# Two GATv2 layers on one core: where a few edges are added up, and which engine divides the sums

## The chip, the cores and the metric

The kernel runs on one core of a Trainium2 chip. The core has five engines that run their own instruction streams and meet at semaphores: PE (TensorE, the matmuls; PEld is its weight load), DVE (VectorE), ACT (ScalarE), POOL (GpSimd, which here issues the indirect DMAs) and SP (SyncE, which issues plain DMAs). The metric is the device time of one execution, in microseconds (us). The kernel before takes 3889.89 us, the median of three runs (3889.52 to 3891.73).

## What is computed

A graph has 6250 nodes with 256 features and 100000 edges, sorted by target. Two GATv2 layers (4 heads of 64) with an ELU between them, a residual and a layer norm; then one GAT layer (8 heads of 32), a residual and a layer norm. Cut to what matters here:

```python
def _gatv2_layer(x, src, dst, n, Wl, Wr, att, b):
    xl = (x @ Wl).reshape(n, H, C)
    xr = (x @ Wr).reshape(n, H, C)
    e = jax.nn.leaky_relu(xl[src] + xr[dst], NEG_SLOPE)
    logits = jnp.einsum('ehc,hc->eh', e, att)
    m = jax.ops.segment_max(logits, dst, num_segments=n)
    ex = jnp.exp(logits - m[dst])
    denom = jax.ops.segment_sum(ex, dst, num_segments=n)
    alpha = ex / (denom[dst] + 1e-16)
    msg = xl[src] * alpha[:, :, None]
    out = jax.ops.segment_sum(msg, dst, num_segments=n)
    return out.reshape(n, H * C) + b
...
h = _gatv2_layer(x, src, dst, n, Wl1, Wr1, att1, b1)
h = jax.nn.elu(h)
h = _gatv2_layer(h, src, dst, n, Wl2, Wr2, att2, b2)
```

In each GATv2 layer every node also has an edge to itself.

## The kernel before

**Blocks.** The nodes are sorted by their number of incoming edges, the largest first, and cut into 49 blocks of 128; a node has a partition. Block b has cols[b] columns, and column j holds the j-th source of each of its nodes. The number of columns falls from block to block: with the node's own row, the blocks have S = 28 at first and 10 at last in the first two layers. Three loops over the 49 blocks follow one another, one for each layer; the first two are calls of layer2 (i = 0 and 1).

**Columnless edges.** In block 0 a few nodes have more edges than cols[0]. These FEW further places a node are the columnless edges: their logits and their share of the sum are worked out for all of them together, an edge to a partition, and brought to their nodes and back by products with two matrices of zeros and ones, node_of and edges_of. few_r (L1513) brings the target's row to the edges; few_logits gives their logits to lg; few_sum (L1293) brings the weights to the edges (few_w, L1298), weighs the edges' rows on DVE (L1303 to L1307) and adds them to block 0's sum `acc` with a last matmul (L1311).

**One block of a GATv2 layer.** POOL gathers a row of the table for each node and column (L1235), one indirect DMA to a column, into tiles `g` of up to nine columns; there are nine such tiles, so POOL can be some blocks ahead, until it has to wait for a tile that PE has not read yet. own() gives the node's own two rows (layer 1: a transpose and two products on PE, `pl` and `pr`, copied by ACT; layer 2: loaded, copied by ACT). attend(b) has three DVE instructions for each tile: `z` (L1504, L1505) and the sum over a head's features into `lg` (L1506). weights() takes the largest logit of each head on DVE (`top`, L1374), and then ACT does an exponential a head with the sum of its results (`wt` and `den`, L1381). DVE takes the reciprocal (`den`, L1571). weighted_sum multiplies the rows by the weights: most columns on DVE (L1411), the last few on ACT, one instruction a column and head (L1410). PE adds the columns up with matmuls by the identity into `acc` in PSUM (L1418). There is one `acc` (pool ps1 with one buffer), and there are two buffers of `wt`.

**The end of a block lies in the next one.** In iteration b the loop does the gathers of block b+1 and own(b+1), then attend(b), then end(b-1): DVE multiplies block b-1's `acc` by its reciprocals in one instruction (L1537), adds the bias (layer 1, L1542) and hands on to finish1 or finish2. finish1 has the ELU on ACT (L1609 to L1612) and DVE (L1617), a transpose, products, two copies on ACT (L1624) and two stores on SP; finish2 the residual, the statistics and the layer norm (L1464), then a transpose, a product, copies and a store.

**Order.** Every engine does its instructions in the order in which the program has them. On ACT an iteration is thus: the copies of own(b+1), the exponentials of b, a copy of the weights that ACT itself uses (`by`), own's other copy, the spots of the sources (L1530, layer 1), end(b-1)'s part, L1410, and the copies at the end of finish. On DVE: `z` and `lg`, `top`, in the first blocks of layer 1 the sorting of sources (sort_sources), L1537 and what follows, `den`, L1411. On PE: own(b+1), the sum of b, then finish of b-1.

In block 0, few_r stands after all of the block's `z` and `lg`, and few_sum directly after the block's sum: `more` is called at the end of weighted_sum.

Of the kernel before, what the change touches and what calls it, by code (L numbers as in the profile page):

```python
# [26 lines left out]
F32 = mybir.dt.float32  # L27
# [8 lines left out]
P = 128  # L36
# [1106 lines left out]
def tile_by_degree(  # L1143
# [3 lines left out]
    nc = tc.nc  # L1147
    N, F = x.shape
    H2, D2 = att1.shape
    H1, _, D1 = w3.shape  # L1150
    NB = -(-N // P)
# [3 lines left out]
    W2 = H2 * (D2 + 1)  # L1155
# [9 lines left out]
    def per_head(t, H):  # L1165
        return t.rearrange("p (h d) -> p h d", h=H)
# [24 lines left out]
    node_of = consts.tile([P, P], F32, name="node_of")  # L1191
# [204 lines left out]

        return (wt, None), add_up

    def weighted_sum(ps, rows, cut, wts, H, width, between, more=None):

        wt, by = wts
        acc = ps.tile([P, F], F32, name="acc")
        S = cut[-1][1]
        for g, (s0, s1) in zip(rows, cut):
            n = s1 - s0
            g4 = g[:, :n, : H * width].rearrange("p t (h d) -> p t h d", h=H)[:, :, :, : F // H]
            m = n - by.shape[1] if by is not None and s1 == S else n
            for t in range(m, n):
                for h in range(H):
                    nc.scalar.mul(g4[:, t, h, :], g4[:, t, h, :], by[:, t - m, h : h + 1])  # L1410
            nc.vector.tensor_mul(  # L1411
                g4[:, :m], g4[:, :m],
                wt[:, s0 : s0 + m, :].unsqueeze(3).to_broadcast([P, m, H, F // H]),
            )
            if s0 == 0:
                between()
            for t in range(n):
                nc.tensor.matmul(  # L1418
                    acc, ident, g4[:, t], start=s0 + t == 0, stop=s0 + t == S - 1 and not more
                )  # L1420
        if more:
            more(acc, wt, S)
        return acc

    def added_up(work, prod, rows, cut, wts, H, width, between):
# [40 lines left out]
    def layer2(i, table, of, width, start, own, finish, follow):  # L1466

        with ExitStack() as es:
            zp = es.enter_context(tc.tile_pool(name=f"z{i}", bufs=1))
            work = es.enter_context(tc.tile_pool(name=f"work{i}", bufs=3))
            ps = es.enter_context(tc.tile_pool(name=f"ps{i}", bufs=2, space=PSUM))
            ps1 = es.enter_context(tc.tile_pool(name=f"ps1{i}", bufs=1, space=PSUM))
            pst = es.enter_context(tc.tile_pool(name=f"pst{i}", bufs=2, space=PSUM))
            at = ps1.tile([P, W2], F32, name="at")
            nc.scalar.copy(at, att[i])
            state = {}  # L1480

            def gather(b):
                first = EARLY[b] if b in begun else 0
                rows, cut = begun.pop(b) if first else row_tiles(b, 1)
                gather_rows(b, rows, cut, 1, table, of, width, first, cols[b])
                if b == 0:
                    gather_few(table, i, width)
                state[b] = [rows, cut]

            later = []  # L1490

            def ready(b):
                pr, put = own(work, ps, pst, b, state[b][0][0][:, 0, :W2])
                state[b].append(pr)
                later.append(put)

            def attend(b):
                rows, cut, xr = state.pop(b)
                S = cols[b] + 1
                lg = work.tile([P, CM + 1, H2], F32, name="lg")  # L1500
                for g, (s0, s1) in zip(rows, cut):
                    n = s1 - s0
                    z = zp.tile([P, T, W2], F32, name="z")[:, :n, :]
                    nc.vector.tensor_max(z, g[:, :n, :W2], xr[:, None, :].to_broadcast([P, n, W2]))  # L1504
                    nc.vector.tensor_mul(z, z, at[:, None, :].to_broadcast([P, n, W2]))  # L1505
                    nc.vector.reduce_sum(  # L1506
                        lg[:, s0:s1, :], z.rearrange("p t (h d) -> p t h d", h=H2), axis=AX.X
                    )
                if b == 0:
                    own_r = work.tile([P, W2], F32, name="few_own", bufs=1)  # L1510
                    nc.scalar.copy(own_r, xr)
                    po = pst.tile([P, W2], F32, name="few_r", tag="tp")
                    nc.tensor.matmul(po, node_of, own_r, start=True, stop=True)  # L1513
                    none(po)
                    z = zp.tile([P, T, W2], F32, name="z")[:, 0, :]
                    nc.vector.tensor_max(z, few_row[:, :W2], po)
                    nc.vector.tensor_mul(z, z, at)
                    few_lg = work.tile([P, H2], F32, name="few_lg", bufs=1)
                    nc.vector.reduce_sum(few_lg, per_head(z, H2), axis=AX.X)
                    few_logits(work, pst, lg, few_lg, H2)  # L1520
                    if i == 0:
                        nc.vector.tensor_copy(few_at[:, 1:], few_row[:, W2 : W2 + 1])
                few = min(S // 3, cut[-1][1] - cut[-1][0] - 1) if b + 1 < NB else 0
                wt, new = weights(work, ps, lg, S if b else S + FEW, H2, few, S)
                while later:
                    later.pop()()
                if i == 0:
                    for g, (s0, s1) in zip(rows, cut):
                        s = max(s0, 1)
                        nc.scalar.copy(spots[:, b, s - 1 : s1 - 1], g[:, s - s0 : s1 - s0, W2])  # L1530
                    if 0 < b <= len(EARLY):
                        sort_sources(work, pst, b - 1)
                return rows, cut, wt, new

            def end(b, acc, den):
                h = work.tile([P, F], F32, name="h")
                nc.vector.tensor_mul(  # L1537
                    per_head(h, H2), per_head(acc, H2),
                    den.unsqueeze(2).to_broadcast([P, H2, D2]),
                )  # L1540
                if i == 0:
                    nc.vector.tensor_add(h, h, bias[0])  # L1542
                return finish(work, pst, b, h)

            for b in range(3):
                if (i, b) not in loaded:
                    start(b)
            if i == 0:
                find_few(work, pst)
            gather(0)  # L1550
            ready(0)
            later.pop()()
            if i == 0:
                none(state[0][2])
            acc, den, rest = None, None, None
            for b in range(NB):
                if b + 3 < NB:
                    start(b + 3)
                if b + 1 < NB:
                    gather(b + 1)  # L1560
                if b + 2 == NB:
                    follow()
                if b + 1 < NB:
                    ready(b + 1)
                rows, cut, wt, new = attend(b)
                if b:
                    rest = end(b - 1, acc, den)
                if i == 0:
                    nc.vector.tensor_add(x1[:, b, :], x1[:, b, :], bias[1])
                den = new()  # L1570
                nc.vector.reciprocal(den, den)  # L1571

                last = []

                def between():
                    if b:
                        last.append(rest())

                acc = weighted_sum(
                    ps1, rows, cut, wt, H2, D2 + 1, between,  # L1580
                    b == 0 and (lambda acc, wt, S: few_sum(
                        work, pst, acc, wt, S, H2, D2 + 1, False)),
                )
                if i == 0 and b + 1 < NB:
                    none(state[b + 1][2])
                if last:
                    last[0]()
            end(NB - 1, acc, den)()()

    def none(t):  # L1590

# [87 lines left out]
    with ExitStack() as es:  # L1679
        work = es.enter_context(tc.tile_pool(name="work3", bufs=3))  # L1680
        ps = es.enter_context(tc.tile_pool(name="ps3", bufs=3, space=PSUM))
# [59 lines left out]
        acc, den, puts, rest = None, None, {}, None  # L1741
        for b in range(NB):
# [4 lines left out]
            rows, cut, wt, new = attend(b)  # L1747
            if b:
                rest = end(b - 1, acc, den)
            den = new()  # L1750
            nc.vector.reciprocal(den, den)

            def between():
                if b:
                    puts[b - 1] = rest()

            acc = added_up(work, prod, rows, cut, wt, H1, D1, between)
            if b == 0:
                more = ps.tile([P, F], F32, name="few_acc", tag="tp")
# [33 lines left out]
```

## Time and profile before

| | us |
|---|---|
| median of three runs | 3889.89 |
| the profiled execution | 3880.55 |
| its span, first to last instruction | 3878.7 |
| first instruction of block 0's sum, layer 1 (L1418) | at 204.06 |
| last division (L1537), layer 2's last block | at 2713.20 |
| mean of one L1537 on DVE, 128x256, x98 | 0.416 |
| mean of one L1410 on ACT, 128x64, x2056 | 0.337 |
| one of four exponentials L1381, x392, and its read of the sum | 0.296 and 0.188 |

The profile is of one execution; its time and its span differ by 1.85 us, which lie around the first and the last instruction. A busy share says how much of the span an engine had an instruction running. "idle before" is the time in which the engine stood before the instructions of a group, and after the arrow stands what released it. "issue" is time in which the engine waited for nothing that the profile shows; "remote" a semaphore whose sender the profile can't tell. In the timeline a row has the start, the duration, the engine, the line and operation, what is written and read, and in brackets how long the engine was idle before and what released it.

### The profile page before, as it was taken

To read this page: it belongs to the slowest core of one execution; us is meant where nothing else is said; L and a number is where in the kernel's file an instruction comes from. 1 tells how busy PE (TensorE), PEld (TensorE's weight loads), DVE (VectorE), ACT (ScalarE), POOL (GpSimd) and SP (SyncE) were. 2 spreads that over 40 slices of the span, in tenths; PEclk is the share of its full clock that TensorE was granted. 3 is DMA by queue.
4 is the path that set the end of the run, shared out by engine and by line. 5 is a ranking of instruction groups with operands and counts; after the bars stand their busy time and mean duration, and the time that the engine had idled before them with its cause. 6 is when DMAs were issued, how large, how long until landed. Compare 5 with 4: busy or idle time off the path is not lost.

```text
span 3878.7 us, 23608 instructions
## 1 busy us (share of the span) xinstructions
PE 1481.8 (38%) x5130; PEld 1113.8 (29%) x5130; DVE 2836.2 (73%) x2648; ACT 1091.1 (28%) x4176; POOL 2530.5 (65%) x2613
## 2 busy tenths in 40 slices
PE   6324665556667763355544545554000000000000
PEld 5213444434555542343433433443000000000000
DVE  6228988668888876899876988896676565666665
ACT  3113444334445442243433434443000000000000
POOL 6464666666666645666666666664777777777774
PEclk8656877778788886676666677776555555555555
DMA  8532333333434334333433434442343333333332
GB/s 188 109 92 78 98 104 104 100 99 103 105 102 108 104 79 109 100 106 104 112 107 105 111 107 110 109 111 74 101 108 101 96 97 96 97 97 96 97 97 57
DMA packets 196123, 395.60 MB, mean 102 GB/s; under 512 B 63036, under 2 KB 115514, under 8 KB 195956
## 3 DMA queue, kind: packets, MB, share of 16 engines
q0 software_dynamic: 122048, 338.04, 33.2%
q1 hardware_dynamic: 66226, 54.22, 5.1%
q10 hardware_dynamic: 7698, 1.74, 0.4%
q8 instruction: 45, 0.74, 0.1%
q14 instruction: 106, 0.87, 0.1%
HBM read 353.82 MB, written 40.42 MB: 102 GB/s over the span
## 4 chain that ended last, share of the span: by engine, by line
issue 20%; POOL 20%; DVE 13%; PE 10%; another core or an unknown queue 6%; ACT 5%; DMA 1%; DVEq 0%; POOLq 0%; ACTq 0%
POOL g L1235 18%; PE acc L1418 6%; DVE z L1505 4%; DVE z L1504 4%; DVE lg L1506 3%; PE pm L1362 3%; ACT g L1410 2%; ACT wt L1381 2%; DVE g L1411 1%; POOL out L1733 1%; DMA g<-xl_d,near_r 1%; DVE weighted L1433 1%; ACT xT L1357 0%; PE pt L1355 0%
## 5 line engine op out<-in xcount | busy, mean ns | idle before, releaser
L1235 POOL DMA_INDIRECT g<-xl_d,near_r x1569 | 1487.4, 948 | 858.7 <-issue 454.3
L1418 PE MATMUL acc<-g,ident 128*128 128x256 f32 x3408 | 1015.9, 461 | 765.3 <-issue 282.7
L1418 PEld LDWEIGHTS acc<-g,ident 128*128 128x128 f32 x3408 | 774.4, 234 | 1004.2 <-issue 522.3
L1235 POOL DMA_INDIRECT g<-whs_d,near_r x766 | 793.2, 1036 | 284.2 <-issue 250.0
L1410 ACT ACTIVATE g<-g,by 128x64 f32<-128x64 f32 x2056 | 545.1, 337 | 316.1 <-issue 310.8
L1504 DVE TENSOR_TENSOR z<-g,pr 128x1820 f32<-128x1820 f32 (+4 forms) x234 | 497.1, 2125 | 19.1 <-DMA g<-xl_d,near_r 10.0
L1505 DVE TENSOR_TENSOR z<-z,at 128x1820 f32<-128x1820 f32 (+4 forms) x234 | 497.4, 2126 | 8.0
L1506 DVE TENSOR_REDUCE lg<-z 128x28 f32<-128x1820 f32 (+4 forms) x234 | 497.3, 2125 | 8.1
L1442 DVE TENSOR_REDUCE acc_v<-weighted 128x256 f32<-128x4096 f32 (+15 forms) x49 | 343.7, 7014 | 16.5 <-remote 8.3
L1411 DVE TENSOR_TENSOR g<-g,wt 128x1792 f32<-128x1792 f32 (+8 forms) x234 | 348.4, 1505 | 2.9
L1391 ACT ACTIVATE wt<-lg 128x128 f32<-128x128 f32 (+17 forms) x49 | 14.0, 285 | 851.0 <-DVE top L1374 391.5
L1703 DVE TENSOR_TENSOR lg<-g,s_r 128x56 f32<-128x56 f32 (+4 forms) x111 | 22.1, 213 | 315.1 <-DMA g<-whs_d,near_r 272.5
L1357 ACT COPY xT<-pt 128x256 f32<-128x256 f32 x147 | 54.9, 374 | 688.5 <-remote 342.2
L1433 DVE TENSOR_TENSOR weighted<-g,wt 128x1792 f32<-128x1792 f32 (+4 forms) x111 | 226.6, 2056 | 0.1
L1571 DVE RECIPROCAL den<-den 128x4 f32<-128x4 f32 x98 | 17.4, 177 | 212.9 <-ACT wt L1381 165.2
L1381 ACT ACTIVATE wt<-lg,top 128x19 f32<-128x19 f32 (+14 forms) x392 | 116.0, 296 | 190.8 <-DVE lg L1506 74.3
L1362 PE MATMUL pm<-wcat,xT 128*128 128x260 f32 x392 | 136.0, 505 | 56.3 <-ACT xT L1357 49.8
L1362 PE MATMUL pm<-wh_cat,xT 128*128 128x272 f32 x196 | 77.5, 531 | 183.8 <-ACT xT L1357 95.5
L1537 DVE TENSOR_TENSOR h<-acc,den 128x256 f32<-128x256 f32 x98 | 40.7, 416 | 126.2 <-remote 112.8
L1362 PEld LDWEIGHTS pm<-wcat,xT 128*128 128x128 f32 x392 | 94.8, 255 | 90.5 <-ACT xT L1357 64.6
L1362 PEld LDWEIGHTS pm<-wh_cat,xT 128*128 128x128 f32 x196 | 42.8, 242 | 203.0 <-ACT xT L1357 104.7
L1362 PE MATMUL pl<-wcat,xT 128*128 128x260 f32 x196 | 64.0, 455 | 55.5 <-issue 40.4
(232 smaller groups left out, 1548.4 us busy)
## 6 DMA issues: line engine op xcount, KB each, us to landing
g<-xl_d,near_r POOLq DMA_INDIRECT x1569
g<-whs_d,near_r POOLq DMA_INDIRECT x766
whs_d<-row SPq DMA_DIRECT2D x49, 132.0 KB
xl_d<-xl SPq DMA_DIRECT2D x49, 130.0 KB
xl_d<-row SPq DMA_DIRECT2D x49, 130.0 KB
xr_d<-row SPq DMA_DIRECT2D x49, 130.0 KB
two<-xl_d SPq DMA_DIRECT2D x49, 130.0 KB
two<-xr_d SPq DMA_DIRECT2D x49, 130.0 KB
```

Of the source, the lines that this page charges most:

```text
L1235: nc.gpsimd.indirect_dma_start(out=g[:, j + own - s0, :width], out_offset=None, in_=table, in_offset=source(of, b, j),)
L1357: nc.scalar.copy(xT, pt)
L1362: nc.tensor.matmul(pm, xT[:, c, :], w[:, c, :], start=c == 0, stop=c == 1)
L1381: nc.scalar.activation(wt[:, :, h], lg[:, :S, h], AF.Exp, bias=top[:, h : h + 1], accum_out=den[:, h : h + 1],)
L1410: nc.scalar.mul(g4[:, t, h, :], g4[:, t, h, :], by[:, t - m, h : h + 1])
L1411: nc.vector.tensor_mul(g4[:, :m], g4[:, :m], wt[:, s0 : s0 + m, :].unsqueeze(3).to_broadcast([P, m, H, F // H]),)
L1418: nc.tensor.matmul(acc, ident, g4[:, t], start=s0 + t == 0, stop=s0 + t == S - 1 and not more)
L1433: nc.vector.tensor_mul(prod[:, s0 - base : s1 - base, :].rearrange("p t (h d) -> p t h d", h=H), g[:, :n, :F].rearrange("p t (h d) -> p t ...
L1442: nc.vector.reduce_sum(part, prod[:, : s1 - base, :].rearrange("p s f -> p f s"), axis=AX.X)
L1504: nc.vector.tensor_max(z, g[:, :n, :W2], xr[:, None, :].to_broadcast([P, n, W2]))
L1505: nc.vector.tensor_mul(z, z, at[:, None, :].to_broadcast([P, n, W2]))
L1506: nc.vector.reduce_sum(lg[:, s0:s1, :], z.rearrange("p t (h d) -> p t h d", h=H2), axis=AX.X)
```

## The change

Two things change in the first two layers.

First, few_sum is no longer called at the end of block 0's weighted_sum, but in iteration 1, by a function middle() that attend calls after the logits and before weights(). Block 0's weights are kept for it (few_wt). The product few_r and the copy that it needs go from behind block 0's logits to ahead of them.

Second, the division of block b-1's sum goes from one DVE instruction in end(b-1), after `top`, to four ACT instructions, one a head, in scaled(), which middle() calls ahead of the exponentials of block b. The last block's is called after the loop.

```diff
-    def weighted_sum(ps, rows, cut, wts, H, width, between, more=None):
+    def weighted_sum(ps, rows, cut, wts, H, width, between, more=False):
...
-        if more:
-            more(acc, wt, S)
         return acc
...
-            def attend(b):
+            def attend(b, middle):
                 rows, cut, xr = state.pop(b)
                 S = cols[b] + 1
                 lg = work.tile([P, CM + 1, H2], F32, name="lg")
+                if b == 0:
+                    own_r = work.tile([P, W2], F32, name="few_own", bufs=1)
+                    nc.scalar.copy(own_r, xr)
+                    po = pst.tile([P, W2], F32, name="few_r", tag="tp")
+                    nc.tensor.matmul(po, node_of, own_r, start=True, stop=True)
...
                 if b == 0:
-                    own_r = work.tile([P, W2], F32, name="few_own", bufs=1)
-                    nc.scalar.copy(own_r, xr)
-                    po = pst.tile([P, W2], F32, name="few_r", tag="tp")
-                    nc.tensor.matmul(po, node_of, own_r, start=True, stop=True)
                     none(po)
...
+                middle()
                 few = min(S // 3, cut[-1][1] - cut[-1][0] - 1) if b + 1 < NB else 0
                 wt, new = weights(work, ps, lg, S if b else S + FEW, H2, few, S)
...
-            def end(b, acc, den):
+            def scaled(acc, den):
                 h = work.tile([P, F], F32, name="h")
-                nc.vector.tensor_mul(
-                    per_head(h, H2), per_head(acc, H2),
-                    den.unsqueeze(2).to_broadcast([P, H2, D2]),
-                )
+                for k in range(H2):
+                    nc.scalar.mul(
+                        per_head(h, H2)[:, k, :], per_head(acc, H2)[:, k, :], den[:, k : k + 1]
+                    )
+                return h
+
+            def end(b, h):
...
-                rows, cut, wt, new = attend(b)
+                h = []
+
+                def middle():
+                    if b == 1:
+                        few_sum(work, pst, acc, few_wt, cols[0] + 1, H2, D2 + 1, False)
+                    if b:
+                        h.append(scaled(acc, den))
+
+                rows, cut, wt, new = attend(b, middle)
                 if b:
-                    rest = end(b - 1, acc, den)
+                    rest = end(b - 1, h[0])
+                else:
+                    few_wt = wt[0]
...
                 acc = weighted_sum(
-                    ps1, rows, cut, wt, H2, D2 + 1, between,
-                    b == 0 and (lambda acc, wt, S: few_sum(
-                        work, pst, acc, wt, S, H2, D2 + 1, False)),
+                    ps1, rows, cut, wt, H2, D2 + 1, between, b == 0,
                 )
...
-            end(NB - 1, acc, den)()()
+            end(NB - 1, scaled(acc, den))()()
```

In the order of the instructions this means: on DVE the four instructions of few_sum stand behind the logits of block 1 in place of ahead of them; on PE the transposes of block 2 and its products `pl` and `pr` (layer 1) stand ahead of few_w in place of behind it; on ACT the copy for few_w stands behind the copy of block 2's transposed rows. POOL and SP have the instructions of before in the order of before.

More of the change, by code (lines that the diff above doesn't have):

```diff
@@ L1554, in layer2 @@
                 none(state[0][2])
-            acc, den, rest = None, None, None
+            acc, den, rest, few_wt = None, None, None, None
             for b in range(NB):
```

## The prediction

> **What bounds the kernel now.** I read the page first, then the tables of waits, then the timeline of both GATv2 layers block by block. A block is 128 nodes, 49 to a layer. The page's groups give the prices:
>
> ```profile
> span 3878.7 us, 23608 instructions
> PE 1481.8 (38%) x5130; PEld 1113.8 (29%) x5130; DVE 2836.2 (73%) x2648; ACT 1091.1 (28%) x4176; POOL 2530.5 (65%) x2613
> L1410 ACT ACTIVATE g<-g,by 128x64 f32<-128x64 f32 x2056 | 545.1, 337 | 316.1 <-issue 310.8
> L1537 DVE TENSOR_TENSOR h<-acc,den 128x256 f32<-128x256 f32 x98 | 40.7, 416 | 126.2 <-remote 112.8
> ```
>
> DVE is the busiest engine, so taking 98 instructions of 0.416 us from it looks like 41 us. The table of waits and the timeline say otherwise:
>
> ```profile
> DVE den L1571 <- ACT wt L1381: 165.2, 61, 12.1
> DVE den L1571 <- issue: 47.8, 34, 9.5
> DVE few_weight L1303 <- remote: 86.3, 2, 68.7
> ```
>
> and, of a late block of layer 1 in the timeline,
>
> ```profile
> 1119.19 0.94 POOL L1235 DMA_INDIRECT g<-xl_d,near_r  x1 [3.52 <-remote]
> 1121.85 0.26 DVE L1374 TENSOR_REDUCE top<-lg 128x4 f32<-128x64 f32 x1
> 1122.03 0.41 DVE L1537 TENSOR_TENSOR h<-acc,den 128x256 f32<-128x256 f32 x1
> 1125.09 0.38 ACT L1357 COPY xT<-pt 128x256 f32<-128x256 f32 x1
> 1125.35 0.31 ACT L1381 ACTIVATE wt<-lg,top 128x16 f32<-128x16 f32 x1
> 1127.15 0.18 DVE L1571 RECIPROCAL den<-den 128x4 f32<-128x4 f32 x1 [3.91 <-ACT wt L1381]
> ```
>
> The reader is to see that DVE, after `top`, has the division L1537 and a few short instructions, and then stands at `den` L1571 until ACT's four exponentials (1.80 us) are done: 95 waits, 212.9 us together. L1537 lies inside that wait. Where ACT is early (block 2 of layer 2, at 1621) the wait still is 0.42 us. In some 59 of 97 blocks (35 in layer 1, 24 in layer 2) ACT was still at earlier work 1 us before `top` ended, or later; there ACT is what DVE waits for.
>
> Behind ACT's lateness stands POOL. In layer 2:
>
> ```profile
> 1785.36 0.94 POOL L1235 DMA_INDIRECT g<-xl_d,near_r  x1 [3.69 <-remote]
> ...
> 1812.58 0.94 POOL L1235 DMA_INDIRECT g<-xl_d,near_r  x1 [3.54 <-remote]
> 1815.97 0.31 ACT L1381 ACTIVATE wt<-lg,top 128x21 f32<-128x21 f32 x1
> ...
> 1839.72 0.94 POOL L1235 DMA_INDIRECT g<-xl_d,near_r  x1 [3.71 <-remote]
> 1843.11 0.31 ACT L1381 ACTIVATE wt<-lg,top 128x20 f32<-128x20 f32 x1
> ```
>
> POOL issues gathers 1.25 us apart, runs out of buffers, waits some 3.5 us for PE to release one, and resumes. The exponentials start 3.39 us after each resumption (1815.97 - 1812.58 and 1843.11 - 1839.72, and the same for five more blocks), although PE's sums were recorded done 5 to 8 us before it. So, as I read it, PE's results reach the others when POOL pauses, and the pace is POOL's: its gathers times 1.25 us, plus a pause. In layer 1's late blocks it is the same with 5 to 6 us in place of 3.39, and pauses of 3.2 to 3.8 us, while the time from the exponentials to POOL's resumption varies from 14.7 to 17.1 us. The block period there is 21.9 us, and DVE needs 19 to 20 us of it from the exponentials to the next `top`.
>
> **The change part by part.**
>
> *The columnless edges' share, a block later.* Now DVE, having scaled block 0's rows at 208.2, stands until PE has the product `few_w`, behind all of block 0's sums:
>
> ```profile
> 276.95 0.20 DVE L1303 TENSOR_TENSOR few_weight<-few_w,few_hot 128x44 f32<-128x44 f32 x1 [68.75 <-remote]
> 300.85 0.33 DVE L1374 TENSOR_REDUCE top<-lg 128x4 f32<-128x104 f32 x1
> ...
> 1565.98 0.20 DVE L1303 TENSOR_TENSOR few_weight<-few_w,few_hot 128x44 f32<-128x44 f32 x1 [17.55 <-remote]
> ```
>
> Afterwards it does block 1's logits meanwhile (nine instructions, 2.32 and 2.59 us each: 22.8 us). In layer 1 that work ends near 232 (its gathers are issued till 222), and then `few_weight` still waits for PE: acc of block 0, as now until 277, but then also block 2's transposes and the products `pl`, `pr`, which stand ahead of `few_w` in the new order; those ran from 278.5 to 283.9. So few_weight comes near 283.3. Queued behind it on DVE is `top` (284.6); behind the last product (285.5) ACT's divisions and exponentials, with `den` near 289 (DVE sorts meanwhile) against 305.25 now. I take 15.7 us; bounds 0 (if PE comes correspondingly later) and 22.8 (all of the logits). POOL follows: its pause that ends at 314.24 waits for block 1's sums, and the next pauses, 8.7 and 13.4 us, are long too, so POOL shifts with DVE.
>
> In layer 2 `few_w` is there at 1566, before the logits end (1548.5 + 22.8 = 1571.3). `den` comes at 1571.3 + 0.9 for the three small instructions + 1.2 for PE + 1.07 + 1.8 + latencies, 1576.7, against 1591.85: DVE gains 15.2. But there POOL paces: it runs without a stop from 1556 to 1595.75, and its next pauses are 5.66, 4.21, 3.95 and 3.91 us. Down to 3.5 each, these give 3.7 us; without the first, 7.2. I take 5; bounds 3.7 and 15.2.
>
> *The first product sooner.* few_own and few_r move ahead of the logits. DVE's memset on few_r at 196.71 follows its predecessor without a gap, so nothing waits for them now: 0 either way. The cover is DVE's logits; without it they cost 0.38 + 1.23 us a layer.
>
> *ScalarE divides.* 98 DVE instructions go, 392 ACT instructions come, ahead of the exponentials on ACT. One costs 0.337 us (L1410, same shape, scale by a column); 24 in a row took 5.83 us, so four take 0.337 + 3 x 0.243 = 1.07 us. Their source is PSUM, which L1410's isn't; ACT's copies from PSUM (0.374 us, 256 wide) are no slower than from SBUF (0.396 to 0.411, 260 wide). Upper bound 4 x 1.40 = 5.6 us, the pace ACT falls to late in some blocks (0.35 us and 1.05 idle); lower 0.97. I take 1.07, since the exponentials at that very place run at full pace now.
> DVE's 0.416 us saves nothing where it waits at `den`; only blocks 2 and 3 of layer 1, which sort there without a wait, give 0.8 us.
> ACT's 1.07 us is hidden where ACT is idle over 1.1 us before `top` (38 blocks; cover: DVE's logits). In the 59 others it delays `den` and with it all of DVE. If POOL paces, that shifts the exponentials against POOL once and isn't added up, as DVE has 2 to 2.7 us spare in a period. I charge: 2.1 us where a POOL-paced stretch gives way to a DVE-paced one for good (once a layer); 1.6 for two nearly late blocks near layer 2's end; at each layer's last block, where ACT waits for the sum and nothing covers, 1.07 - 0.41 = 0.66, 1.3 for two; 1.07 for the block before layer 2's last: 6 us. Bounds 0 and 59 x 1.07 = 63. Further, ACT's scaling of g ends later before POOL's pause; pauses with four or more such instructions left over are about 0.2 us longer than those with none (3.84 against 3.58, near 880 to 908): at most 35 x 0.2 = 7, I take 3.
>
> The Trainium skill, "ScalarE: Activation LUTs", section "Rules for kernel authors", tells authors to do plain multiplications on VectorE, not ScalarE; these rows agree as to the instruction (1.07 us against 0.416). If the rule held for the whole time, the divisions would cost 98 x 0.65 = 64 us.
>
> The buffers: block 0's `wt` is held a block longer, but its copy comes before block 1's exponentials need theirs, so no wait. POOL's and SP's instructions and DMAs are the same.
>
> **Sum.** -15.7 - 5 - 0.8 + 6 + 3 = -12.5 us. The profiled execution took 3880.55 us (span 3878.7) and would take 3868; the median, 3889.89, stands 9.3 above it, so 3877.4.
>
> **The rivals.**
> *ACT becomes the bound (slower).* If POOL's pause follows PE, which follows ACT, instead of setting both, each late block pays 1.07 us. All 59: +63 - 21.5 = +41, 3931. Layer 1's 35 alone: +37 - 21.5 + 2 = +18, 3908. For it: ACT's g instructions often end at or after POOL's pause (0.87 us after 1115.67). Against: the constant 3.39 us, and a period that follows the gathers. It decides from the point at which the exponentials' delay against POOL passes DVE's spare 2 us. Chance 0.08 + 0.15.
> *The wait only moves.* few_w, behind eight more products, is late by as much as DVE is early; layer 1 gains nothing: -12.5 + 15.7 = +3, 3893. For it: PE signalled nothing for 22 us before 277. Against: from 278.5 on PE ran those products without a stall. Chance 0.13.
> *Both gains whole.* POOL's pauses shrink or drop out when PE's work is there earlier: -15.7 - 15.2 - 0.8 + 6 = -26, 3864. For it: POOL has 92 us of pause above 3.5 us each in layer 1; against: only 19 in layer 2. Chance 0.18.
> *My forecast*, 3877: 0.46.
>
> **How the numbers follow.** The range, 3850 to 3915, reaches from the third rival less 14 us (pauses skipped or added, 3.5 us each, four of them) past the milder form of the first; it leaves out its full form. The likeliest case alone: 3865 to 3890. A measurement can tell 0.2%, 7.8 us. Faster by more: 0.72 of my case, all of the third, 0.51. Slower: the first, a third of the second, 0.28. Within: 0.21.
>
> **What would show it.** Right: few_weight's wait in layer 1 some 50 us (232 to 283), in layer 2 none or nearly; `top` of block 1 near 285 and 1572; no L1537 on DVE, 392 ACT instructions of 0.34 us; waits at `den` longer by about 0.4 us in early-ACT blocks; POOL's pauses still 3.2 to 3.8 us; exponentials 6 to 8 us behind POOL's resumption in layer 1. Wrong: pauses a microsecond longer, block periods of 23 us where they were 21.9, or few_weight after 295.

## The result and the profile after

The changed kernel takes 3868.77 us (median of 6 runs, 3860.47 to 3875.10) against 3889.49 us before (6 runs on the same chip, 3885.55 to 3891.73). The ratio is 0.9946, with a 95% interval of 0.9929 to 0.9962: 21 us, or half a per cent, faster.

The page of the changed kernel's profiled execution (3874.58 us by the clock; span, busy time by engine, and groups, whose columns are busy us, mean ns of one, and idle time before them with what ended it). In its numbering L1539 is ScalarE's division, L1546 and L1660 are the first instruction of end() on DVE in layers 1 and 2, L1585 is the reciprocal `den`, L1411 is ScalarE's scaling of gathered rows and L1419 PE's sum:

```profile
span 3872.7 us, 23945 instructions
PE 1483.9 (38%) x5129; PEld 1106.3 (29%) x5130; DVE 2800.2 (72%) x2550; ACT 1185.3 (31%) x4568; POOL 2533.0 (65%) x2613
L1411 ACT ACTIVATE g<-g,by 128x64 f32<-128x64 f32 x2056 | 559.2, 338 | 454.2 <-issue 450.9
L1660 DVE TENSOR_TENSOR h<-h,near_r 128x256 f32<-128x256 f32 x49 | 20.8, 424 | 146.9 <-ACT h L1539 91.3
L1546 DVE TENSOR_TENSOR h<-h,fixed_r 128x256 f32<-128x256 f32 x49 | 20.7, 422 | 142.5 <-ACT h L1539 76.4
L1539 ACT ACTIVATE h<-acc,den 128x64 f32<-128x64 f32 x392 | 92.2, 331 | 23.5 <-PE acc L1311 17.2
```

The DVE division is gone (2550 instructions for 2648), and 392 ACT instructions of 0.331 us have come. The table of waits of the same execution (us together, times, longest):

```profile
DVE h L1660 <- ACT h L1539: 91.3, 15, 21.8
DVE h L1546 <- ACT h L1539: 76.4, 12, 21.9
DVE few_weight L1303 <- PE few_w L1298: 49.6, 1, 49.6
DVE den L1585 <- ACT wt L1381: 41.2, 48, 1.2
DVE den L1585 <- issue: 38.2, 47, 2.0
```

DVE's stand at `den` shrank from 212.9 to 79.4 us, but it now stands earlier, at the first add of end(), which needs ACT's quotient: 142.5 + 146.9 us idle there. Before, the three places (the division, its adds, `den`) had 126.2 + 4.0 + 1.7 + 212.9 = 344.8 us of idle time; now they have 368.8. So 40.7 us of work left DVE and these waits grew by 24.0; part of that is few_sum's move, which changes them too, and the division's own part is read on chip 2 below.

The timeline of DVE shows the other half of the change:

```profile
286.73 0.20 DVE L1303 TENSOR_TENSOR few_weight<-few_w,few_hot 128x44 f32<-128x44 f32 x1 [49.62 <-PE few_w L1298]
287.58 0.33 DVE L1374 TENSOR_REDUCE top<-lg 128x4 f32<-128x104 f32 x1
...
291.83 0.17 DVE L1585 RECIPROCAL den<-den 128x4 f32<-128x4 f32 x1
...
1567.92 0.19 DVE L1303 TENSOR_TENSOR few_weight<-few_w,few_hot 128x44 f32<-128x44 f32 x1
```

few_weight waits one time, not twice, and between it and `top` the 22.8 us of logits are missing. `den` of block 1 comes at 291.83, where it came at 305.25. This execution began its first layer 5.1 us later than the one before (the first `z` at 168.87 against 163.80, behind a longer wait in the setup), so the gain is 18.5 us. That later start is one reason why the two profiled executions differ by 6 us only, and the medians by 21; the other is that this pair's lead shrinks again in the last blocks, as the table shows next.

How the lead then goes, block by block, is the question of the rest. The table gives the end of `top` in some blocks (0 to 48 are layer 1, 49 to 97 layer 2), counted from the first `z` of its execution, less the same of the kernel it is compared with; a lead is a negative number. Chips and labels are explained below.

```
chip, kernel less kernel                   1      5     46     49     50     56     64     94
1  changed less before                 -18.4  -15.2  -14.7   -8.2  -26.0   -7.8   -5.3  -13.8
3  changed less before                 -18.6  -19.9  -19.2  -15.2  -33.0  -16.9  -16.9  -22.0
3  e6_product_first less before        -23.2  -29.1  -31.1  -27.3  -45.1  -28.7  -28.9  -35.5
2  changed less division alone         -10.0   -9.7   -7.3   -3.9  -14.9  -13.0  -13.0  -13.1
2  changed less later few_sum alone      0.1   -1.3   -0.4    1.6    1.6    3.0    3.0    3.1
```

On chips 1 and 3 layer 1 gains some 18.5 us in one step at block 1. Layer 2 gains another 17.8 us at block 50 and has given nearly all of it back by block 56 to 64. Each row is one pair of executions, and between the blocks shown it swings: on chip 1 the lead is 36.2 us at block 17 and 8.7 at block 19, and it falls from 13.8 at block 94 to 6.4 at the last, 97.

### The profile page after: what moved, and what is told of

It is laid out like the page before. It is cut to its first block, busy times and chain, and to the rows that moved or that the text cites. A ratio compares the mean times of both kernels' runs of the same rounds, so it can differ in the third digit from the quotient of the medians.

```text
span 3872.7 us, 23945 instructions
## 1 busy us (share of the span) xinstructions
PE 1483.9 (38%) x5129; PEld 1106.3 (29%) x5130; DVE 2800.2 (72%) x2550; ACT 1185.3 (31%) x4568; POOL 2533.0 (65%) x2613
## 4 chain that ended last, share of the span: by engine, by line
issue 27%; POOL 22%; PE 15%; DVE 15%; ACT 9%; another core or an unknown queue 9%; DMA 2%; DVEq 0%; SPq 0%; ACTq 0%; POOLq 0%
POOL g L1235 20%; PE acc L1419 11%; ACT g L1411 4%; DVE z L1508 4%; DVE z L1509 4%; DVE lg L1510 3%; PE pm L1362 3%; ACT wt L1381 2%; DVE g L1412 1%; POOL out L1745 1%; ACT h L1539 1%; DMA g<-xl_d,near_r 1%; POOL near L998 1%; ACT xT L1357 1%
## 5 line engine op out<-in xcount | busy, mean ns | idle before, releaser
L1419 PE MATMUL acc<-g,ident 128*128 128x256 f32 x3408 | 1046.7, 470 | 854.1 <-issue 379.0
L1419 PEld LDWEIGHTS acc<-g,ident 128*128 128x128 f32 x3408 | 783.7, 238 | 1110.7 <-issue 554.9
L1411 ACT ACTIVATE g<-g,by 128x64 f32<-128x64 f32 x2056 | 559.2, 338 | 454.2 <-issue 450.9
L1432 DVE TENSOR_TENSOR weighted<-g,wt 128x1792 f32<-128x1792 f32 (+4 forms) x111 | 226.5, 2056 | 0.1
L1362 PE MATMUL pm<-wcat,xT 128*128 128x260 f32 x392 | 114.6, 442 | 49.3 <-ACT xT L1357 31.1
L1660 DVE TENSOR_TENSOR h<-h,near_r 128x256 f32<-128x256 f32 x49 | 20.8, 424 | 146.9 <-ACT h L1539 91.3
L1546 DVE TENSOR_TENSOR h<-h,fixed_r 128x256 f32<-128x256 f32 x49 | 20.7, 422 | 142.5 <-ACT h L1539 76.4
L1362 PEld LDWEIGHTS pm<-wcat,xT 128*128 128x128 f32 x392 | 80.4, 216 | 76.3 <-ACT xT L1357 43.1
L1539 ACT ACTIVATE h<-acc,den 128x64 f32<-128x64 f32 x392 | 92.2, 331 | 23.5 <-PE acc L1311 17.2
```

Source lines behind the costliest of these rows:

```text
L1362: nc.tensor.matmul(pm, xT[:, c, :], w[:, c, :], start=c == 0, stop=c == 1)
L1419: nc.tensor.matmul(acc, ident, g4[:, t], start=s0 + t == 0, stop=s0 + t == S - 1 and not more)
L1432: nc.vector.tensor_mul(prod[:, s0 - base : s1 - base, :].rearrange("p t (h d) -> p t h d", h=H), g[:, :n, :F].rearrange("p t (h d) -> p t ...
L1539: nc.scalar.mul(per_head(h, H2)[:, k, :], per_head(acc, H2)[:, k, :], den[:, k : k + 1])
```

## The experiments

Three chips appear: 1, of the result; 2, on which the kernel before takes 3366 us (3363.5 to 3369.9); and 3, on which it takes 3872 us (3857.4 to 3887.6). Not every kernel ran on every chip. Each ratio is to the kernel before on the same chip, and each edit is shown against the changed kernel. The times expected for e1 and e2 are those of chip 1, so on chip 2 only their differences can be compared. The theories: A, the later few_sum gives the gain, and GpSimd's gathers pace chips 1 and 3, so that the division costs little; B, the work taken off DVE gives it; C, ACT paces the late blocks and each division is paid for.

**The later few_sum alone** (e1 and e9, chip 2). DVE divides, where it did before:

```diff
-                for k in range(H2):
-                    nc.scalar.mul(
-                        per_head(h, H2)[:, k, :], per_head(acc, H2)[:, k, :], den[:, k : k + 1]
-                    )
+                nc.vector.tensor_mul(
+                    per_head(h, H2), per_head(acc, H2),
+                    den.unsqueeze(2).to_broadcast([P, H2, D2]),
+                )
...
-                    rest = end(b - 1, h[0])
+                    rest = end(b - 1, scaled(acc, den))
```

> Only the columnless edges' share moves; DVE divides as before. Theory A (the move gives all, POOL paces, so the division on ACT costs little and gives nothing): 3861 to 3870, at or up to 8 us below the changed kernel. Theory B (freeing DVE of 98 divisions gives a good part of the gain): 3875 to 3885. Theory C (ACT paces the late blocks, each division there costs 1.07 us, and the move gives far more than the result shows): 3810 to 3835.

Measured: 3350.28 us, ratio 0.9954 (0.9940 to 0.9967), 15.4 us less than before. Theory A had 20 to 28 us less than before, too much for this chip, where the wait ahead of few_weight is shorter (below); what parts it from B holds: this half alone is faster than the changed kernel (by 4.7 us, e9 against e12 below), where B has it slower.

**The division alone** (e2 and e10, chip 2). few_sum and the product few_r stay where they were:

```diff
                 def middle():
-                    if b == 1:
-                        few_sum(work, pst, acc, few_wt, cols[0] + 1, H2, D2 + 1, False)
                     if b:
                         h.append(scaled(acc, den))
...
+                if b == 0:
+                    few_sum(work, pst, acc, few_wt, cols[0] + 1, H2, D2 + 1, False)
```

> Only the division moves to ACT; the columnless edges' product and share stand as before. Theory A: 3889 to 3899, no gain and at most 10 us of loss. Theory B: 3865 to 3880. Theory C: 3925 to 3955, some 59 blocks by 1.07 us.

Measured: 3371.73 us, ratio 1.0017 (1.0008 to 1.0026), 6.0 us more than before. The half that takes 98 instructions off DVE makes the kernel slower on this chip, although DVE is its busiest engine: theory B falls for this chip.

**The first product where it was** (e3, chip 2): the changed kernel with few_own and few_r behind block 0's logits again.

```diff
-                if b == 0:
-                    own_r = work.tile([P, W2], F32, name="few_own", bufs=1)
...
                 if b == 0:
+                    own_r = work.tile([P, W2], F32, name="few_own", bufs=1)
...
```

> The changed kernel, but few_r stands behind block 0's logits again. Theory A: no difference from the changed kernel beyond its own scatter of some 7 us either way. If the earlier product matters: slower than the changed kernel by the 1 to 3 us it takes, in each of two layers.

Measured: 3355.56 us, ratio 0.9969 (0.9956 to 0.9981). The changed kernel itself took 0.9968 on this chip (e12, below), so the order of that product moves nothing; and -15.4 + 6.0 = -9.4 against -10.2, so the two halves add up.

**Eight divisions for four** (e4, chip 2): e3 with the four repeated into a tile that nobody reads.

```diff
+                for k in range(H2):
+                    nc.scalar.mul(
+                        per_head(twice, H2)[:, k, :], per_head(acc, H2)[:, k, :], den[:, k : k + 1]
+                    )
```

> The changed kernel with eight ACT divisions a block in place of four; the first four write a tile that nobody reads. Theory A (POOL paces): +2 to +8 us against the changed kernel, with the exponentials about 1 us later behind POOL's resumptions and pauses unchanged within 0.2 us. Theory C (ACT paces): +40 to +63 us, and longer pauses.

Measured: 3363.67 us, ratio 0.9993 (0.9984 to 1.0002), 8.1 us more than e3. The page has the added group, and DVE's stand at `den` in the groups of the two is all but equal (93.3 us in e3):

```profile
L1540 ACT ACTIVATE twice<-acc,den 128x64 f32<-128x64 f32 x392 | 92.6, 333 | 39.0 <-PE acc L1311 39.0
L1590 DVE RECIPROCAL den<-den 128x4 f32<-128x4 f32 x98 | 17.4, 178 | 91.4 <-ACT wt L1381 91.4
```

92.6 us more of ACT's work cost 8.1. Theory C's 1.07 us a block does not hold on this chip: the rest lies in ACT's idle time, while DVE is at its logits.

**The four again, side by side** (e9 to e12, chip 2 once more): few_sum alone, division alone, few_sum alone with its product sooner, and the changed kernel.

> The later few_sum alone, with VectorE dividing as before; the same kernel took 0.9954 of the time before on a chip where the kernel before takes 3366 us. The two sorts of chip seen so far take 3366 us and 3872 to 3890 us for the kernel before. On one of the slower sort, theory A (the move gives the gain, GpSimd paces, the division on ScalarE costs little) expects 19 to 24 us less than before: the changed kernel's 17 to 21 us and the 2 to 6 us that the division costs. Theory B (the division is what gives the gain where GpSimd paces, since VectorE's work counts there) expects less than 12 us of gain here. On a chip of the faster sort both expect 15 us again.

> The division on ScalarE alone, few_sum as before; 6.0 us slower than before on the chip where the kernel before takes 3366 us. On a chip of the slower sort theory A expects 0 to 8 us more than before, theory B 5 to 15 us less. On one of the faster sort both expect 6 us more again.

> The changed kernel beside its parts, on one chip with them. Theory A: its time is that of the later few_sum alone plus what the division alone costs against before, within 3 us. Theory B: it is 5 us or more below the later few_sum alone on a chip of the slower sort.

Measured, with before at 3366.46: e9 3351.37 us, 0.9953 (0.9940 to 0.9967); e10 3371.04 us, 1.0013 (1.0004 to 1.0023); e12 3356.12 us, 0.9968 (0.9957 to 0.9980). The division costs 4.7 us between e9 and e12, and 4.6 between before and e10. The page of e9 (few_sum alone):

```profile
PE 1351.8 (40%) x5129; PEld 1077.0 (32%) x5130; DVE 2834.8 (85%) x2648; ACT 1048.6 (31%) x4176; POOL 2466.6 (74%) x2613
L1411 ACT ACTIVATE g<-g,by 128x64 f32<-128x64 f32 x2056 | 500.0, 334 | 0.0
```

and tables of waits, first of e9 and then of e12 (the changed kernel on the same chip):

```profile
DVE den L1581 <- ACT wt L1381: 51.6, 94, 2.0
```

```profile
DVE den L1585 <- ACT wt L1381: 93.7, 95, 2.0
ACT h L1539 <- PE acc L1311: 38.9, 2, 24.6
DVE h L1660 <- ACT h L1539: 11.0, 4, 7.9
DVE h L1546 <- ACT h L1539: 10.3, 2, 9.2
```

These few lines are the clearest reading of what a division moved off DVE is worth. Nothing else differs between the two kernels but the division; DVE loses 40.7 us of work and gains 42.1 us of waiting at the same reciprocal, 0.46 us a block by the median, since the exponentials that it waits for start when `top` ends, with the division or without it. The 4.7 us that it costs come at few places. In the last row of the table the sort blocks give 1.4 us, and the rest of layer 1 takes 0.9 back; layer 1's end and layer 2's start take 2.1, block 1 of layer 2 another 1.4, where ACT's division stands ahead of the exponentials and waits for few_sum's last product (the 38.9 us of the second fence are two such waits, one a layer); the remaining 1.7 come at and behind layer 2's last blocks. The question of e9's expectation, whether the division helps where GpSimd paces, this chip cannot answer; e6 below bears on it.

What the move is worth on chip 2 is seen against e10, whose table of waits has

```profile
DVE few_weight L1303 <- PE few_w L1298: 21.5, 2, 10.8
```

Two waits of 10.8 us, where chips 1 and 3 have some 69 and 17.6. Removing them gives 10.0 and 11.0 us of lead (fourth row). Of the second, 9.2 us are kept from block 51 to the end; of the first, 7.3 are left late in layer 1 and 3.9 at layer 2's first block. What takes the rest of layer 1's gain on this chip is open. On chip 2 GpSimd pauses for more than 2 us only 13 times (54 us, all in layer 2), against 96 times (434 us) in the changed kernel on chip 1.

**The product of few_sum ahead of block 2's own** (e6 on chip 3, e11 on chip 2): the later few_sum, DVE dividing, and few_w called before ready(b + 1).

```diff
+                if b == 1:
+                    few_pw = few_product(work, pst, few_wt, cols[0] + 1, H2)
                 if b + 1 < NB:
                     ready(b + 1)
...
-                        few_sum(work, pst, acc, few_wt, cols[0] + 1, H2, D2 + 1, False)
+                        few_sum(work, pst, acc, few_wt, cols[0] + 1, H2, D2 + 1, False, few_pw)
```

> The kernel before once more, for its profile on the chip of this call. On a chip where ACT stops between its multiplications (316 us idle in the first profile, at L1410) theories A and C expect POOL's pauses of 3.2 to 3.8 us and late exponentials again; on a chip where it doesn't, both expect DVE to pace, the exponentials to start 0.03 us behind the largest logits in nearly all blocks, and few_weight to stand some 10 us in each layer.

> The columnless edges' share a block later with DVE's division (e1_few_only), and the product few_w with its copy issued ahead of block 2's own products on PE. Theory A: where PE is slow to finish block 0's sums, few_weight comes 4 to 6 us earlier than in the changed kernel, and the time is 8 to 14 us under the changed kernel's; where DVE paces, few_weight doesn't wait either way and the time equals e1_few_only's, 0.9945 to 0.996 of before. Theory B (the division on ACT is a gain): slower than the changed kernel.

> The changed kernel once more, on the chip of this call. Theory A: 0.993 to 0.998 of before; on a chip where DVE paces nearer 0.997, since POOL's pauses give nothing there.

Measured on chip 3, with before at 3871.90 (18 runs; the profiled one, e5, 3880.39, with POOL's pauses and the late exponentials of chip 1 again): e6 3846.24 us, 0.9938 (0.9916 to 0.9959); the changed kernel, e8, 3855.17 us, 0.9954 (0.9940 to 0.9969), 16.7 us less than before. The timeline of e6:

```profile
280.63 0.20 DVE L1308 TENSOR_TENSOR few_weight<-few_w,few_hot 128x44 f32<-128x44 f32 x1 [44.75 <-remote]
```

and of the changed kernel there:

```profile
284.64 0.20 DVE L1303 TENSOR_TENSOR few_weight<-few_w,few_hot 128x44 f32<-128x44 f32 x1 [49.12 <-PE few_w L1298]
```

few_weight comes 4.0 us sooner (4.6 counted from the first `z`), and the kernel beats the changed one by 8.9 us. On chip 2 the place of the product could not count, as few_weight waits for nothing there:

> The later few_sum with its first product ahead of block 2's own products and VectorE dividing. Beside the kernel that differs in the place of the product alone: if the place of the product counts (its few_weight was 4 us earlier than in the changed kernel, 280.6 against 284.6 us) it is 3 to 5 us faster; if it does not, because few_weight is not what block 1's end waits for, both are within 2 us of one another, and what it had on the changed kernel (8.9 us) was the division alone.

Measured: 3350.25 us, 0.9956 (0.9942 to 0.9969), 1.1 us from e9 with ranges that overlap. Against the changed kernel it is 5.9 us faster, which is the division. So this version beat both kernels on both sorts of chip. How its 8.9 us on chip 3 divide between the product and the division was not separated by a run, but the two profiles, of one execution each, bear on it: the lead of e6 over the changed kernel is 4.6 us at block 1, 11.9 at block 21 and 11.3 at block 48; in layer 2 it is 12.1 at block 49 and, after swings up to block 55, 11.9 at block 56 and 13.6 at block 94. From end to end of these long stretches, with the division on DVE in one kernel and on ACT in the other, their distance changes by less than 2 us. So no gain from the division is seen where GpSimd paces, as theory B has it, and little cost. The 7 us that e6 wins between block 1 and block 21 are not explained.

**More gathers** (e7, chip 3): the changed kernel with one more gather in each block but the first of layers 1 and 2, into a tile of its own that nobody reads.

```diff
+                if b:
+                    spare = work.tile([P, W2 + 1], F32, name="spare", bufs=2)
+                    nc.gpsimd.indirect_dma_start(
+                        out=spare[:, :width], out_offset=None, in_=table, in_offset=source(of, b, 0),
+                    )
```

> The changed kernel with one more gather a block in the first two layers (96 in all, each 1.25 us of POOL, into a tile that nobody reads). Theory A: where ACT stops between its multiplications and the late blocks follow POOL, +50 to +110 us against the changed kernel; where DVE paces, under +12. Theory C (ACT paces the late blocks): under +20 us on either kind of chip.

Measured: 4000.21 us, 1.0336 (1.0303 to 1.0369), 145 us more than the changed kernel: more than any theory expected. It was not run on chip 2. The pages, e7's and then the changed kernel's on that chip:

```profile
span 3983.5 us, 24027 instructions
PE 1514.1 (38%) x5130; PEld 1126.1 (28%) x5130; DVE 2802.2 (70%) x2550; ACT 1187.5 (30%) x4568; POOL 2629.8 (66%) x2709
```

```profile
span 3859.2 us, 23946 instructions
PE 1470.4 (38%) x5130; PEld 1102.1 (29%) x5130; DVE 2800.2 (73%) x2550; ACT 1179.5 (31%) x4568; POOL 2535.3 (66%) x2613
```

DVE's and ACT's work is the same, POOL has 96 instructions more, and the profiled spans differ by 124.3 us, 1.29 us for each; the pitch of a gather is 1.25. The medians differ by more, 1.51 us for each; where the further 20 us come from is open. POOL's pauses of over 2 us shrank little to make room: 94 of them, 409 us, against 98 in the same stretch, 419. By block the growth is uneven: 13.5 us from block 62 to 71, none from block 89 to 96. Over the two layers a gather more on POOL is a gather more in the time, or somewhat more: POOL sets the pace of these layers on this chip, though not of every block, while it is busy for 66% of the span only, less than DVE. What the page calls idle on POOL is a pause that comes once a block and stays. The run does not part POOL's issuing from the transfers that each gather starts.

With that, the division on chip 3 can be read. The timeline of the changed kernel there, a block of layer 2:

```profile
1799.29 0.95 POOL L1235 DMA_INDIRECT g<-xl_d,near_r  x1 [3.73 <-remote]
...
1802.67 0.94 ACT L1539 ACTIVATE h<-acc,den 128x64 f32<-128x64 f32 x4
1803.47 0.34 ACT L1381 ACTIVATE wt<-lg,top 128x21 f32<-128x21 f32 x1
1803.65 0.42 DVE L1660 TENSOR_TENSOR h<-h,near_r 128x256 f32<-128x256 f32 x1 [2.02 <-ACT h L1539]
...
1826.43 0.95 POOL L1235 DMA_INDIRECT g<-xl_d,near_r  x1 [3.37 <-remote]
```

and of the same block in the kernel before (e5):

```profile
1818.39 0.95 POOL L1235 DMA_INDIRECT g<-xl_d,near_r  x1 [3.52 <-remote]
...
1821.79 0.31 ACT L1381 ACTIVATE wt<-lg,top 128x21 f32<-128x21 f32 x1
...
1845.56 0.94 POOL L1235 DMA_INDIRECT g<-xl_d,near_r  x1 [3.67 <-remote]
```

The division starts 3.38 us after POOL resumed, where the exponentials started 3.40 us after it before; the exponentials are 0.80 us later. ACT is late here and DVE waits for it. Yet from block 56 to 67 the lead over the kernel before stays between 16.78 and 16.87 us: twelve blocks, each with four divisions on a late ACT, and not 0.1 us of period. From this resumption to the next POOL takes 27.14 us, and 27.17 between the same two in the kernel before. In layer 1 the lead is 17.5 us at block 21 and 19.2 at block 46. Theory C falls on this chip, by the blocks that it was made for. On chip 1 it is less clear: there POOL's pauses became longer in such blocks (below, under "Pauses longer by 3 us").

## Why the prediction was right

The forecast was 12.5 us less, 3877 us, and faster; 20.7 us less, 3868.8, was measured, inside the range. On chip 3 it was 16.7. The direction and the mechanism were right; that the sum came as near as it did is partly luck, since one term was too small, another much too large, and several us stay unexplained.

*The mechanism.* That the gain is few_sum's move and not DVE's 41 us, that POOL paces, and that the division on ACT costs a little, held: e1 and e9 gain more than the changed kernel and e2 and e10 lose, on chip 2; on chip 3 e7 pays for each gather, and e6, which divides on DVE, is ahead. On chips 1 and 3 the halves were not run alone.

*Layer 1, 15.7 us.* Measured 18.5 at `den` on chip 1 (the prediction's own times for `den`, 289 against 305.25, give 16.3). few_w behind block 2's products came 4.7 us later than at its old place (117.86 against 113.15 us, both from the first `z`), where I had 6.3; and `top` follows at once. The step is right, its size 2.8 us short. The step holds to block 46 on chip 3 (19.2); on chip 1 it is 14.7 by then.

*Layer 2, 5 us.* This term was too large, and its lower bound of 3.7 too high. DVE gained 17.8 us at block 50 on both chips, a little more than the 15.2 said, and gave back all but 1.7 of it by block 56 on chip 3; on chip 1 the lead was 2.9 us smaller at block 64 than at 49. POOL's first pauses there are 5.81, 4.37, 4.13 and 4.22 us on chip 1, where I let 5.66, 4.21, 3.95 and 3.91 shrink to 3.5 each: they did not shrink, and that sentence of the step failed. Where POOL seldom pauses, on chip 2, 9.2 of 11.0 us stayed.

*The division, 6 us.* 4.6 to 6.0 us on chip 2, by four comparisons (e2, e10, e3 less e1, e12 less e9). Its size for one block was right (0.80 us from the first division to the first exponential, 0.94 to the end of the last, 1.07 said), and so were its kinds of places, but for block 1 of layer 2 (1.4 us on chip 2), which it did not name. What the divisions cost in all on chips 1 and 3 was not measured, so that 6 us is confirmed on the other sort of chip only. That 59 late blocks do not add up was the step on which the sign hung, and the twelve blocks of chip 3 show it.
The Trainium skill, "ScalarE: Activation LUTs", section "Rules for kernel authors", keeps plain multiplications on VectorE; on chip 2 the runs agree in direction, with 4.6 to 6.0 us for the kernel that broke it, less than a tenth of the 64 us of the rule taken at full price.

*Pauses longer by 3 us.* Open. Their sum hides it: POOL's pauses of over 2 us sum to 235.5 and 198.8 us in the two layers on chip 1 (243.1 and 201.2 before), and to 221.1 and 198.1 on chip 3 (240.5 and 197.4), but layer 1's sum fell because some of its first pauses had been waits for block 1's late sum. In the 20 pauses of blocks 21 to 40, where the term was expected, POOL stands 74.0 us on chip 1 against 68.4 before, and the stretch takes 422.8 us against 417.8; on chip 3 it is 68.8 against 67.7, and 418.2 against 418.0. So in the profiled execution on chip 1 the term is there with 5 us, more than the 3 charged, and on chip 3 it is next to nothing. Whether the division makes those pauses longer on chip 1, or that execution had them for another reason, no run here tells.

*The sum.* With this term and layer 2 at zero, as on chip 3, and layer 1 and the division at their sizes, the sum by my own steps is -18.5 - 0.8 + 5 = -14; the medians say -20.7 and -16.7. The few us between are of the size of the swings from block to block, where one pause of 8 to 15 us falls into another block (chip 3: the lead goes from 18.2 at block 80 to 27.0 at block 81 and back to 13.3 at block 83). What sets these was not found.

*The profiled execution against the median, 9.3 us.* It stood below the median before and above it after (3874.58 against 3868.77). So its offset did not carry over, and the 3868 forecast for the profiled execution missed; the 12.5 us between the medians do not rest on it.

*First product sooner, 0.* Right (0.9969 for e3, 0.9968 for e12).

*The rivals.* "ACT becomes the bound" would have taken 3908 to 3931; the constant lead on chip 3 and e4 speak against it. "The wait only moves" is refuted by `den` at 291.83. "Both gains whole" comes near layer 2 on chip 2, and fits layer 2 on neither chip 1 nor 3.

*The marks.* few_weight's wait was 49.6 us, to 286.7 in place of 283 on an execution that began 5.1 us later; none in layer 2; `top` of block 1 at 287.6 and 1569; exponentials 5.2 to 7.7 us after POOL's resumption in late layer 1; all as said or near it. So was the longer wait at `den`: in the 28 blocks where ACT was early before and after on chip 1, it grew by 0.46 us by the median, and on chip 3 as much (34 blocks). That the total at `den` still fell on chip 1, from 212.9 to 79.4 us, comes from the late blocks, where the add ahead of it now waits for ACT first. POOL's pauses, said to stay at 3.2 to 3.8 us, were 3.0 to 4.2 in blocks 21 to 40 on chip 1 (3.0 to 3.8 before).

## What to carry to other kernels

A stall in front of work that does not need what is waited for is worth looking for first: moving it behind that work gave this gain. Taking work off the busiest engine gave nothing here, since that engine waits right behind it for another; look at the next wait in its order before counting the instructions. And an engine that is two thirds busy can set the pace if its pauses do not shrink: add one instruction a block to it and see whether the time grows by its pitch.

## What the chips showed unexpectedly

The same kernel takes 3366 us on one chip and 3872 to 3890 us on two others. The granted TensorE clock differs little (0.695 in e9's profile on chip 2; 0.665 and 0.668 before on chips 1 and 3), and a gather takes 0.948 us on chips 1 and 2 alike. What differs is how engines stand between instructions that follow one another: ScalarE's 2056 scalings have no idle time before them on chip 2, and 454.2 us on chip 1 in the changed kernel, ended by nothing that the profile shows. On chips 1 and 3 ACT begins late in most blocks (55 of 98 on chip 3, over 0.2 us behind `top`, in the kernel before); on chip 2 in none of e9's. What the change gains at the start of layer 2 is mostly kept on chip 2 and lost within a few blocks on chips 1 and 3, so a tuning step can be worth something on one sort of chip and nothing on another. Why the engines stand was not tried.
